# Layer 0 reads z and x with two neighbouring tokens per partition, and x for its moments in 32 KB per partition

## The chip, the cores and the metric

The kernel runs on one core of a Trainium2 chip. The metric is the device time of one execution in microseconds (us). Ten executions of the kernel before have a median of 3439.86 us (3437.83 to 3440.95).

## The reference

The input `x` is (1, 128, 256, 256): 128 rows s of 256 tokens i with 256 channels, in float32 (33.5 MB). Two attention layers are added to it in turn, each on a group-normalised input (32 groups of 8 channels, moments over all tokens). The change touches layer 0, which has a second input z, (256, 256, 128), also 33.5 MB:

```python
x = x + _L0_conv_ref(_gn(x), z, ...)
# in _L0_conv_ref, with 8 heads of 32 channels:
m_norm = layer_norm(m, ln_m_w, ln_m_b)
z_norm = layer_norm(z, ln_z_w, ln_z_b)
b = (z_norm @ Wb.T).transpose(0, 3, 1, 2)[:, None]     # a bias for each head, query i and key j
gate = sigmoid(m @ Wg.T + bg)
scores = einsum('bsihc,bsjhc->bshij', q, k) * scale + b
p = softmax(scores); o = einsum('bshij,bsjhc->bsihc', p, v) * gate
return o @ Wo.T + bo
```

The tokens of a row are exchangeable in the attention as long as queries, keys, bias and output use one order. Layer 1 is an attention limited to a band of 16 tokens to either side, so there the order of tokens matters.

## The kernel before, in words

`fast_kernel` does the work; a general kernel stands behind it for unusual inputs and isn't run here. It has three parts.

**The prelude** (lines 990 to 1140) works on z and on the moments of x. `z_front(b, i0)` (line 1048) loads a tile `zt` of 32 queries by 128 keys: partition p holds key b * 128 + p, and for each of 32 queries one run of 128 channels, 512 bytes. VectorE takes the moments of each query's channels (16 BATCH_NORM_STATS2, L1054), then the variance is scaled on VectorE (L1062) and GpSimd raises it to the power -1/2 (`zrs`, L1063). `z_back` (line 1068) transposes the tile on TensorE (L1077), ScalarE copies it (L1079), TensorE projects it to the heads (L1082); of every two tiles the result is turned back (L1092, `ps_k`), multiplied by `zrs` on VectorE in four pieces (L1098), biased on GpSimd (L1102) and exponentiated by ScalarE into `eb` (L1103), which is (128 keys, 8 heads, 2 key blocks, 256 queries). There are 16 such tiles, z0 to z15; `zt` has three buffers. `x_block(j)` (line 1109) loads 16 rows of x at once (4 MB, `xa`, two buffers): partition p holds tokens p and 128 + p of every row, 32 runs of 1 KB. VectorE takes the moments of pairs of groups (L1113, 16 instructions). The eight blocks are xa0 to xa7; `x_moments` (line 1116) merges them after the last.

The program's order of loads on SyncE's queue is z0, xa0, z1, z2, xa1, z3, xa2, z4, z5, xa3, z6, xa4, z7, z8, xa5, z9, xa6, z10, z11, xa7, z12 to z15. On each engine the order of the prelude's instructions is set by the framework's planner, from the costs it expects and the data each instruction needs, and then stays fixed. The buffers of the layer loop reuse the prelude's memory, so that its first load of x is issued after the last exponential into `eb`.

**Layer 0** goes through x in 64 pairs of rows, in an order written out by hand. `Pair` loads two rows (`xt`, L1179, five buffers), again token p and 128 + p of each row on partition p; it is normalised, transposed, projected to q, k, v and gate; `scores` and `add_bias` multiply the exponentials by `eb` (L1290); `apply`, `gate`, `out_row` and `keep_row` produce the new rows. Every 8 rows are stored to `x1` in HBM (L1360), and their moments taken for layer 1. `rows` is the access that lays token b * 128 + p on partition p.

**Layer 1** reads `x1` in pairs of rows (L1557) and writes `out`.

Of the kernel before, what the change touches and what calls it, by code (L numbers as in the profile page):

```python
# [10 lines left out]
AF = mybir.ActivationFunctionType  # L11
# [5 lines left out]
P = 128  # L17
# [4 lines left out]
def bcast(ap, axis, n):  # L22

    ap = ap.unsqueeze(axis)
    shape = list(ap.shape)
    shape[axis] = n
    return ap.broadcast_to(shape)
# [746 lines left out]
def fast_kernel(  # L774
# [25 lines left out]
    nc = tc.nc  # L800
# [7 lines left out]
    NB = I // P  # L808
# [94 lines left out]
    def rows(ap, s0, n):  # L903
        return ap[s0 : s0 + n].rearrange("s (b p) c -> p (s b) c", p=P)


    GA = min(16, S)

    eb = const.tile([P, H, NB, I], F32, name="eb")
# [9 lines left out]
    for a in range(KC):  # L919
        for h in range(H1):  # L920
            n = P // H1
# [11 lines left out]
    for h in range(H1):  # L933
        n = P // H1
# [22 lines left out]
    def group_pairs(src, g):  # L957

        return src[:, :, g * GE : (g + 2) * GE].rearrange("p n (h e) -> p n e h", h=2)
# [24 lines left out]
    with tc.tile_pool(name="pre", bufs=2) as pre, tc.tile_pool(  # L984
# [51 lines left out]

        IB, IS = 32, 64
        zjobs = [(b, i) for b in range(NB) for i in range(0, I, IB)]  # L1040
        wbz = pre1.tile([P, 4, 4, H], F32, name="wbz")
        nc.vector.memset(wbz, 0.0)
        for j in range(4):
# [2 lines left out]
        def z_front(b, i0):  # L1046

            nonlocal zrs
            zt = pre.tile([P, IB, CZ], F32, name="zt", tag="zt", bufs=3)
            nc.sync.dma_start(zt, z[i0 : i0 + IB, b * P : (b + 1) * P, :].rearrange("i p c -> p i c"))  # L1050

            st = pre.tile([P, IB, 3], F32, name="zst", tag="zst")
            for i in range(0, IB, 2):
                nc.vector.bn_stats(  # L1054
                    st[:, i : i + 2, :].rearrange("p i f -> p (i f)"),
                    zt[:, i : i + 2, :].rearrange("p i c -> p c i"),
                )
            at = i0 % IS
            if at == 0:
                zrs = pre.tile([P, IS], F32, name="zrs", tag="zrs", bufs=3)  # L1060
            rs = zrs[:, at : at + IB]
            nc.vector.tensor_scalar(rs, st[:, :, 2], 1.0 / CZ, 1e-5, ALU.mult, ALU.add)  # L1062
            nc.gpsimd.tensor_tensor(rs, rs, mhalf[:, :IB], ALU.pow)  # L1063
            return zt, zrs

        def z_back(b, i0, zt, rs):
            nonlocal ps_b
            at = i0 % IS
            if at == 0:
                ps_b = pps.tile([P, 512], F32, name="ps_b", tag="bias", bufs=1)  # L1070
            for j in range(at // 16, (at + IB) // 16):
                zTs = []
                for g in range(4):
                    ps_t = pps.tile([P, 512], F32, name="ps_t", tag="zT", bufs=3)
                    i = (4 * j + g) * 4 - at
                    for a in range(4):
                        nc.tensor.transpose(ps_t[:, a * P : (a + 1) * P], zt[:, i + a, :], ident)  # L1077
                    zT = pre.tile([P, 512], F32, name="zT", tag="zT", bufs=10)
                    nc.scalar.copy(zT, ps_t)  # L1079
                    zTs.append(zT)  # L1080
                for g in range(4):
                    nc.tensor.matmul(  # L1082
                        ps_b[32 * g : 32 * (g + 1), :], wbz[:, j].rearrange("p a h -> p (a h)"), zTs[g],
                        start=(j == 0), stop=(j == 3),
                    )
            if at + IB < IS:
                return
            bT = pre.tile([P, 512], F32, name="bT", tag="bT")
            nc.scalar.copy(bT, ps_b)
            ps_k = pps.tile([P, 4, 4, 4, H], F32, name="ps_k", tag="keys", bufs=1)  # L1090
            for a in range(4):
                nc.tensor.transpose(  # L1092
                    ps_k[:, a].rearrange("p g j h -> p (g j h)"), bT[:, a * P : (a + 1) * P], ident
                )
            bt = pre.tile([P, IS, H], F32, name="bt", tag="bt")
            for j in range(4):
                q = slice(j * 16, (j + 1) * 16)
                nc.vector.tensor_tensor(  # L1098
                    bt[:, q, :].rearrange("p (g a) h -> p g a h", g=4), ps_k[:, :, :, j, :].rearrange("p a g h -> p g a h"),
                    bcast(rs[:, q].rearrange("p (g a) -> p g a", g=4), 3, H), ALU.mult,  # L1100
                )
            nc.gpsimd.tensor_tensor(bt, bt, bcast(bz_r, 1, IS), ALU.add)  # L1102
            nc.scalar.activation(  # L1103
                eb[:, :, b, i0 - at : i0 - at + IS], bt.rearrange("p i h -> p h i"), AF.Exp
            )

        zrs = ps_b = None

        def x_block(j):
            xa = pre.tile([P, GA * NB, C], F32, name="xa", tag="xa")  # L1110
            nc.sync.dma_start(xa, rows(x, j * GA, GA))
            for g in range(0, G, 2):
                nc.vector.bn_stats(st0[:, j, g : g + 2, :].rearrange("p g f -> p (g f)"), group_pairs(xa, g))  # L1113

# [15 lines left out]
        for n, job in enumerate(zjobs):  # L1130
            front = z_front(*job)
            if behind is not None:
                z_back(*behind)
            behind = (*job, *front)
            if nx < nga and nx * 12 <= n * nga:
                x_block(nx)
                nx += 1
                if nx == nga:
                    M0, R0 = x_moments()
        assert nx == nga  # L1140
        z_back(*behind)


# [7 lines left out]
    x1 = [dram.tile([GB, I, C], F32, name=f"x1_{j}") for j in range(S // GB)]  # L1151
# [9 lines left out]
    with tc.tile_pool(name="l0", bufs=2) as sb, tc.tile_pool(  # L1161
# [10 lines left out]
        class Pair:  # L1172


            def __init__(self, p):
                self.p = p
                self.oT = {}
                self.xt = sb.tile([P, NT, C], F32, name="xt", tag="xt", bufs=5)
                nc.sync.dma_start(self.xt, rows(x, 2 * p, 2))  # L1179


            def centre(self):
# [169 lines left out]
            def keep_row(self, r):  # L1352
                s = 2 * self.p + r
                nc.vector.tensor_tensor(
                    xo[:, (s % GB) * NB : (s % GB + 1) * NB, :], self.ps_y.rearrange("p (b c) -> p b c", b=NB),
                    self.xt[:, r * NB : (r + 1) * NB, :], ALU.add,
                )
                if (s + 1) % GB == 0:
                    j = s // GB
                    nc.sync.dma_start(x1[j].rearrange("s (b p) c -> p (s b) c", p=P), xo)  # L1360
                    moments_of(xo, j)

        xo = None
        later = []

        def moments_of(src, j):

            new = st1 if j == 0 else sm.tile([P, G, 3], F32, name="gst", tag="gst", bufs=2)
            for g in range(0, G, 2):
                later.append(lambda g=g: nc.vector.bn_stats(  # L1370
                    new[:, g : g + 2, :].rearrange("p g f -> p (g f)"), group_pairs(src, g)))
            if j == 0:
                return
            d = sm.tile([P, G], F32, name="gd", tag="gd", bufs=2)
            d2 = sm.tile([P, G], F32, name="gd2", tag="gd2", bufs=2)
            each = float(GB * NB * GE)

            def merge():
                nc.vector.tensor_sub(d, new[:, :, 1], st1[:, :, 1])
                nc.vector.scalar_tensor_tensor(d2, d, each * j / (j + 1), d, ALU.mult, ALU.mult)  # L1380
                nc.vector.tensor_add(d2, d2, new[:, :, 2])
                nc.vector.tensor_add(st1[:, :, 2], st1[:, :, 2], d2)
                nc.vector.scalar_tensor_tensor(
                    st1[:, :, 1], d, 1.0 / (j + 1), st1[:, :, 1], ALU.mult, ALU.add
                )

            later.append(merge)
# [375 lines left out]
@with_exitstack  # L1763
def mixer_kernel(ctx, tc, *args):

    nc = tc.nc
    keep = ctx.enter_context(tc.tile_pool(name="verdict", bufs=1))
    verdict = keep.tile([1, 1], mybir.dt.int32, name="verdict")
    fast_kernel(tc, *args, verdict)
    again = nc.values_load(verdict[0:1, 0:1], min_val=0, max_val=1)  # L1770
    with tc.If(again > 0):
        general_kernel(tc, *args)
# [53 lines left out]
```

## Time and profile before

| | |
|---|---|
| median of 10 executions | 3439.86 us |
| the profiled execution | 3440.28 us, its span 3438.5 us |
| busy: TensorE, VectorE, GpSimd, ScalarE | 3259.1, 2020.2, 1983.0, 1454.9 us |
| z tiles: start of the first pass on VectorE | 27.57 us |
| starts of the eight x passes on VectorE | 40.30, 67.08, 91.42, 118.19, 133.29, 159.92, 184.06, 210.81 us |
| end of the last of them | 220.45 us |
| first load of x for layer 0 issued | 269.40 us |
| first scores of layer 0 | 308.84 us |
| read from and written to HBM | 188.82 MB, 68.75 MB |

The profile is of one execution. In its slices the span is cut in 40 equal parts of 86 us; a digit is a busy share in tenths. A group line gives the start, the length, the engine, the line, what is written from what, and in brackets how long the engine had been idle and what ended the wait. The prelude takes about a tenth of the span; the layer loops are TensorE's.

### The profile page before, as it was taken

To read this page: it belongs to the slowest core of one execution; us is meant where nothing else is said; L and a number is where in the kernel's file an instruction comes from. 1 tells how busy PE (TensorE), PEld (TensorE's weight loads), DVE (VectorE), ACT (ScalarE), POOL (GpSimd) and SP (SyncE) were. 2 spreads that over 40 slices of the span, in tenths; PEclk is the share of its full clock that TensorE was granted. 3 is DMA by queue.
4 is the path that set the end of the run, shared out by engine and by line. 5 is a ranking of instruction groups with operands and counts; after the bars stand their busy time and mean duration, and the time that the engine had idled before them with its cause. 6 is when DMAs were issued, how large, how long until landed. Compare 5 with 4: busy or idle time off the path is not lost. (4 is left out here: it accounts for less than half of the span.)

```text
span 3438.5 us, 81082 instructions
## 1 busy us (share of the span) xinstructions
PE 3259.1 (95%) x35158; PEld 2047.7 (60%) x35158; DVE 2020.2 (59%) x3218; ACT 1454.9 (42%) x2065; POOL 1983.0 (58%) x1385
## 2 busy tenths in 40 slices
PE   5565999999999999999999999799999999999998
PEld 3332555555555555555555555476767676777776
DVE  5872666666666666666666666366644444444455
ACT  2332444444444444444444444244444444444443
POOL 2445777777777777777777776333333333333332
PEclk8787999999999999999999999899999999999999
DMA  9971122122212221222122211221111212121211
GB/s 281 318 214 31 48 72 72 48 72 72 72 48 72 72 72 48 72 72 72 48 72 72 72 48 50 70 64 52 58 57 55 60 51 64 51 64 52 64 57 52
DMA packets 246941, 262.88 MB, mean 76 GB/s; under 512 B 46288, under 2 KB 213072, under 8 KB 246448
## 3 DMA queue, kind: packets, MB, share of 16 engines
q1 hardware_dynamic: 246576, 257.61, 26.0%
q8 instruction: 278, 4.55, 0.7%
q14 instruction: 87, 0.71, 0.1%
HBM read 188.82 MB, written 68.75 MB: 75 GB/s over the span
## 5 line engine op out<-in xcount | busy, mean ns | idle before, releaser
L1295 POOL TENSOR_TENSOR eboth<-e 128x512 f32<-128x512 f32 x512 | 639.7, 1271 | 401.8 <-DVE e L1290 401.8
L1290 DVE TENSOR_TENSOR e<-ps_sc,eb 128x1024 f32<-128x1024 f32 x512 | 603.2, 1220 | 338.8 <-ACT ps_sc L1281 253.7
L1281 ACT ACTIVATE ps_sc<-ps_sc 128x1024 f32<-128x1024 f32 x512 | 492.8, 1006 | 507.4 <-PE ps_sc L1274 507.4
L1615 POOL TENSOR_TENSOR e<-e,bw 128x384 f32<-128x384 f32 x256 | 258.9, 1033 | 443.9 <-ACT e L1613 443.9
L1576 PE MATMUL ps_p<-xgT,w_in 128*128 128x512 f32 x1024 | 469.6, 601 | 0.1
L1568 POOL TENSOR_TENSOR xt<-xt,bout_r 128x1024 f32<-128x1024 f32 x64 | 152.0, 2376 | 384.1 <-PE ps_x L1565 384.1
L1668 DVE TENSOR_TENSOR yo<-ps_y,xt 128x512 f32<-128x512 f32 x128 | 88.3, 690 | 378.6 <-PE ps_y L1664 378.6
L1576 PEld LDWEIGHTS ps_p<-xgT,w_in 128*128 128x128 f32 x1024 | 188.9, 190 | 200.0 <-issue 166.8
L1274 PE MATMUL ps_sc<-qT,kT 32*128 32x256 f32 x4096 | 293.8, 400 | 1.6 <-ACT kT L1244 1.6
L1240 PE MATMUL ps_p<-xnT,wq 128*128 128x512 f32 x512 | 255.7, 622 | 20.8 <-POOL xnT L1228 20.8
L1305 PE MATMUL ps_ov<-e,v 128*32 128x256 f32 x4096 | 274.1, 385 | 0.5 <-DVE oT L1319 0.5
L1240 PE MATMUL ps_p<-xgT,wg 128*128 128x512 f32 x512 | 253.9, 618 | 0.0
L1664 PE MATMUL ps_y<-w_out,oT 128*128 128x256 f32 x1024 | 248.6, 386 | 2.6 <-DVE oT L1649 2.6
L1347 PE MATMUL ps_y<-wo,oT 128*128 128x256 f32 x1024 | 243.8, 381 | 7.0 <-POOL oT L1337 7.0
L1347 PEld LDWEIGHTS ps_y<-wo,oT 128*128 128x128 f32 x1024 | 195.6, 191 | 88.0 <-issue 59.5
L1255 PE MATMUL ps_v<-wv,xnT 128*128 128x256 f32 x1024 | 242.1, 379 | 0.0
L1240 PE MATMUL ps_p<-xnT,wk 128*128 128x512 f32 x512 | 241.8, 595 | 0.0
L1274 PEld LDWEIGHTS ps_sc<-qT,kT 32*128 32x128 f32 x4096 | 185.4, 184 | 94.1 <-issue 70.5
L1591 PE MATMUL ps_v<-w_in,xgT 128*128 128x256 f32 x1024 | 231.8, 379 | 0.0
L1646 DVE RECIPROCAL rv<-odd 128x256 f32<-128x256 f32 x128 | 224.4, 1753 | 4.4
L1591 PEld LDWEIGHTS ps_v<-w_in,xgT 128*128 128x128 f32 x1024 | 194.4, 190 | 53.5 <-issue 30.1
L1255 PEld LDWEIGHTS ps_v<-wv,xnT 128*128 128x128 f32 x1024 | 189.6, 190 | 50.9 <-issue 31.1
(164 smaller groups left out, 5025.8 us busy)
## 6 DMA issues: line engine op xcount, KB each, us to landing
xa<-in_x_dram SPq DMA_DIRECT2D x8, 4096.0 KB
xt<-in_x_dram SPq DMA_DIRECT2D x64, 512.0 KB
rvb<-rsum SPq DMA_DIRECT2D x256, 128.0 KB
x<-xo SPq DMA_DIRECT2D x16, 2048.0 KB
xt<-x SPq DMA_DIRECT2D x64, 512.0 KB
out_dram<-yo SPq DMA_DIRECT2D x63, 512.0 KB
rs_r<-rs_d SPq DMA_DIRECT2D x64, 256.0 KB
rs_d<-lrs SPq DMA_DIRECT2D x64, 2.0 KB
```

Of the source, the lines that this page charges most:

```text
L1240: nc.tensor.matmul(ps, w[:, k, m * P : (m + 1) * P], getattr(self, src)[:, k, :], start=(k == 0), stop=(k == KC - 1),)
L1255: nc.tensor.matmul(self.ps_v[:, b * C : (b + 1) * C], self.xnT[:, k, t * P : (t + 1) * P], wv[:, k, :], start=(k == 0), stop=(k == KC - 1),)
L1274: nc.tensor.matmul(self.pss[q // 2][:, q % 2, b, :], self.kT[rs, c, r * I + b * P : r * I + (b + 1) * P], self.qT[rs, c, r * I : (r + 1) * I],
L1281: nc.scalar.activation(self.pss[a], self.pss[a], AF.Exp)
L1290: nc.vector.tensor_tensor(e, pss[a], eb[:, h : h + 2], ALU.mult)
L1295: nc.gpsimd.tensor_tensor(t, es[a][:, :, 0, :], es[a][:, :, 1, :], ALU.add)
L1305: nc.tensor.matmul(ov[q * D0 : (q + 1) * D0, :], self.v[:, r, b, h * D0 : (h + 1) * D0], es[q // 2][:, q % 2, b, :], start=(b == 0), stop= ...
L1347: nc.tensor.matmul(self.ps_y[:, b * C : (b + 1) * C], self.oT[r][:, k, b * P : (b + 1) * P], wo[:, k, :], start=(k == 0), stop=(k == KC - 1),)
L1576: nc.tensor.matmul(ps, w_in[:, k, n * C + m * P : n * C + (m + 1) * P], self.xgT[:, k, :], start=(k == 0), stop=(k == KC - 1),)
L1591: nc.tensor.matmul(ps[:, b * C : (b + 1) * C], self.xgT[:, k, t * P : (t + 1) * P], w_in[:, k, 2 * C : 3 * C], start=(k == 0), stop=(k == ...
L1615: nc.gpsimd.tensor_tensor(e[:, q], e[:, q], bcast(bw.rearrange("p b w -> p (b w)"), 1, KC), ALU.mult)
L1664: nc.tensor.matmul(ps[:, b * C : (b + 1) * C], self.oT[r][:, k, b * P : (b + 1) * P], w_out[:, k, :], start=(k == 0), stop=(k == KC - 1),)
```

## The change

Partition p now holds the neighbouring tokens 2p and 2p + 1 in layer 0, where it held p and 128 + p. In z, a tile takes 16 query pairs: its 32 columns are keys 2p and 2p + 1 of one query, for 16 queries of one parity (b), so that a run has 256 channels, 1 KB. A query's place in `eb` follows: even queries come first, then odd ones. The rows of x that the layer loop loads, and the rows of `x1` that it stores, have runs of two tokens, 2 KB. For the moments, which need no order, a block of 16 rows is laid out flat, 32 KB per partition. The bytes, tiles, buffers and the numbers of instructions on the compute engines stay. Layer 1 reads `x1` as before, since `x1` in HBM has the same content.

```diff
+        z_rows = z.rearrange("(u t) (p b) c -> t p u (b c)", t=NB, b=NB)
...
-            nc.sync.dma_start(zt, z[i0 : i0 + IB, b * P : (b + 1) * P, :].rearrange("i p c -> p i c"))
+            nc.sync.dma_start(
+                zt.rearrange("p (u b) c -> p u (b c)", b=NB), z_rows[b, :, i0 // NB : (i0 + IB) // NB, :]
+            )
...
             nc.scalar.activation(
-                eb[:, :, b, i0 - at : i0 - at + IS], bt.rearrange("p i h -> p h i"), AF.Exp
+                eb[:, :, :, b * P + (i0 - at) // NB : b * P + (i0 - at + IS) // NB],
+                bt.rearrange("p (u b) h -> p h b u", b=NB), AF.Exp,
             )
...
-            nc.sync.dma_start(xa, rows(x, j * GA, GA))
+            nc.sync.dma_start(xa, x[j * GA : (j + 1) * GA].rearrange("s i c -> (s i) c").rearrange("(p n) c -> p n c", p=P))
...
-                nc.sync.dma_start(self.xt, rows(x, 2 * p, 2))
+                nc.sync.dma_start(
+                    self.xt.rearrange("p (s b) c -> p s (b c)", b=NB),
+                    x[2 * p : 2 * p + 2].rearrange("s (p b) c -> p s (b c)", b=NB),
+                )
...
-                    nc.sync.dma_start(x1[j].rearrange("s (b p) c -> p (s b) c", p=P), xo)
+                    nc.sync.dma_start(
+                        x1[j].rearrange("s (p b) c -> p s (b c)", b=NB), xo.rearrange("p (s b) c -> p s (b c)", b=NB)
+                    )
```

## The prediction

> **What bounds the kernel now.** I read the slices of the page first. The transfer engines are full in the first slices alone, and there TensorE is half idle:
>
> ```profile
> PE   5565999999999999999999999799999999999998
> DMA  9971122122212221222122211221111212121211
> GB/s 281 318 214 31 48 72 72 48 72 72 72 48 72 72 72 48 72 72 72 48 72 72 72 48 50 70 64 52 58 57 55 60 51 64 51 64 52 64 57 52
> ```
>
> So the change, which alters transfers, can act in the prelude (z and the moments of x, some 300 us) and hardly elsewhere. Second, the table by stretches (columns after the length: busy us of PE, PEld, DVE, ACT, POOL, then TensorE clock, DMA share, GB/s). I cut the prelude where VectorE ends the last x block (220.45) and where the first x load of the layer loop is issued (269.40):
>
> ```profile
> 27.57:220.45 192.88, 116.91 (x630) 69.90 (x630) 147.68 (x357) 65.02 (x113) 72.56 (x18) 0.78 1.07 319
> 220.45:269.40 48.95, 30.86 (x174) 17.01 (x174) 26.98 (x90) 17.56 (x31) 29.58 (x7) 0.86 0.25 68
> 320.00:2160.00 1840.00, 1832.27 (x14228) 1060.04 (x14224) 1214.43 (x1945) 817.48 (x1014) 1438.28 (x1010) 1.00 0.23 63
> ```
>
> Stretch one: transfers always busy, VectorE 77%. Stretch two: transfers a quarter busy, no engine full, so a chain of waits. The layer loop: TensorE 99.6%, transfers 23%. Third, transfers of a stretch with only x under way (56 to 66 us), and of one with only z (42 to 47 us):
>
> ```profile
> DMA packets 3243, 3.45 MB, mean 345 GB/s; under 512 B 14, under 2 KB 3099, under 8 KB 3243
> DMA packets 723, 1.45 MB, mean 290 GB/s; under 512 B 16, under 2 KB 16, under 8 KB 723
> ```
>
> The 1 KB runs of x move at 345 GB/s, the 512 B runs of z at 290 (their records hold four runs each). A z tile is 128 x 32 x 512 B = 2.097 MB, 7.23 us; an x block 4.194 MB, 12.16 us. Last, VectorE in order of time, over one x block and the next, and its waits in 17 to 270 us (total, times, longest):
>
> ```profile
> 67.08 9.63 DVE L1113 BATCH_NORM_STATS2 st<-xa 128x6 f32<-128x512 f32 x16 [5.39 <-DMA xa<-in_x_dram]
> 76.63 5.39 DVE L1054 BATCH_NORM_STATS2 zst<-zt 128x6 f32<-128x256 f32 x16
> 85.09 0.29 DVE L1098 TENSOR_TENSOR bt<-ps_k,zrs 128x128 f32<-128x128 f32 x1 [3.06 <-PE ps_k L1092]
> 85.30 0.17 DVE L1062 TENSOR_SCALAR zrs<-zst 128x32 f32<-128x32 f32 x1
> 85.39 0.28 DVE L1098 TENSOR_TENSOR bt<-ps_k,zrs 128x128 f32<-128x128 f32 x1
> 91.02 0.49 DVE L1098 TENSOR_TENSOR bt<-ps_k,zrs 128x128 f32<-128x128 f32 x2 [5.35 <-POOL zrs L1063]
> 91.42 9.67 DVE L1113 BATCH_NORM_STATS2 st<-xa 128x6 f32<-128x512 f32 x16
> ...
> DVE bt L1098 <- POOL zrs L1063: 25.9, 6, 5.4
> DVE st L1113 <- DMA xa<-in_x_dram: 17.7, 3, 7.1
> DVE bt L1098 <- PE ps_k L1092: 12.1, 4, 5.5
> ```
>
> VectorE is the thread that leads to the end of stretch one, and its order is fixed. It waits for x three times, for the z projection ps_k (behind a z transfer) three times there, and for GpSimd's power (5.44 us each), which no transfer shortens. A faster stream is therefore worth much less than the time it saves on the transfer engines.
>
> **What the Trainium skill says.** "DMA: Bandwidth & Descriptors", section Why small descriptors are slow: each packet costs a fixed few cycles beside its beats, so short runs lose rate. The trace agrees: 290 against 345. Same page, section Measured: 341 GB/s for 1 MB, 425 for 16 MB. No x or z transfer here reaches that; the nearest, a 1 MB load in 8 KB rows (sums, 2189.2 to 2193 us), moves at 358 with the engines 95.7% busy, 374 if full. Same page, section Latency and other measured facts: row pitches of large powers of two cut the rate (half at 4 MiB); no transfer of before shows it.
>
> **The change, part by part.** Times are VectorE's starts of x blocks xa0 to xa7, before: 40.30, 67.08, 91.42, 118.19, 133.29, 159.92, 184.06, 210.81.
>
> *z in 1 KB runs.* Half the runs; I price them as today's 1 KB runs of x: 345 GB/s, 6.08 us instead of 7.23. Bounds: no gain (7.23), and 425 GB/s (4.93).
>
> *x blocks as 32 KB per partition.* Bounds: no gain (12.16), and 425 GB/s (9.87). I take 400, the mean of 374 and 425: 10.5 us. 4096 runs become 128, so SyncE's issue of 5.7 to 10.2 us a block should shrink; SyncE then waits at the buffers (two for x, three for z) instead, which holds nothing up, as the walk below shows.
>
> *Carried forward along VectorE.* Tile z0 lands 27.57 - 1.15 = 26.4. xa0: the old gap of 12.73 less 1.66, so 37.5. Before xa1 come z1 and z2, so xa1 lands 37.5 + 2 x 6.08 + 10.5 = 60.2; VectorE is free at 37.5 + (61.69 - 40.30) = 58.9, so it still waits 1.3: 60.2, 6.9 earlier. Tile z3 lands 66.3; its projection took 85.09 - 74.39 = 10.7 from landing to VectorE, so 77.0; the power and its wait follow as before (91.42 - 85.09 = 6.33): xa2 at 83.3, 8.1 earlier. From xa2 to xa3 26.77 us are two z tiles, 9.6 of x and two powers in a row on GpSimd (10.83): no transfer in it, 110.1. To xa4 15.10 likewise: 125.2. To xa5 26.63 less the 5.24 waited for x: 146.6 (the stream has it at 138.7). To xa6 24.14 less the 2.87 waited for ps_k: 167.8 (z9 lands 144.8, projected by 155.5; VectorE comes at 161.5). To xa7 26.75, again two powers: 194.6 against 210.81. **Gain 16.2 us.** Buffers: the block after next needs its VectorE pass done; xa4, the closest, needs xa2's pass (92.9) and has its turn in the stream at 105.6.
>
> *Stretch two, 48.95 us: unchanged.* After the last block come the merging of moments, two matmuls, a power, three more powers in a row (16.22 us), bias, exponential, the last projection and power. The last z tile is issued when z12 is released (237.9) and would land some 1.2 us sooner, but what follows it stands behind GpSimd until 254.5: no gain.
>
> *The exponential into eb* (L1103) writes pieces of 32 instead of 64, the same 512 elements: 1.13 us as now. If a piece doubled it, two of the eight lie in the tail: +2.3 us. The bias layout is otherwise the same size and its readers (L1290) have the same shapes.
>
> *x in pairs for the layer, 64 loads, and x1 stores, 16, in 2 KB runs.* The first load is on the path: 0.524 MB at 400 instead of 345 GB/s saves 0.2 us of the 4.45 from its issue (269.40) to GpSimd's start (273.85). The others, x1's stores included, lie under TensorE; waits for transfers between 400 and 2100 us sum to 1.2 us. If that cover went, the other 63 loads would bring 63 x 0.2 = 13 us more. The last x1 store overlaps the final moments. Layer 1 reads x1 as before.
>
> Sum: 16.2 + 0.2 = 16.4 us. The profiled execution was 3440.28 us (span 3438.5), the median 3439.86; 3440.28 - 16.4 = 3423.9, against the median 3423.5.
>
> **Rivals.** (a) *Only one transfer gains.* x at 12.16 with z at 6.08: the same walk gives xa1 63.5, xa2 86.6, xa5 149.9 and a gain of 12.9; z alone unimproved about the same: 3427. Were neither to gain, or the tail take it back: 3440. For it: the z runs' own spacing doubles; the 8 KB load shows only 374.
> (b) *The order changes.* Outside the layer loops the planner arranges each engine's instructions by the times it expects; before, it set the bias multiplies (L1098) ahead of the next x block. If it expects the new x earlier, blocks move ahead and the power waits (5.35, 4.55, 5.35, 4.91) hide. Then the stream decides: after xa5 at 138.7 come z9, x, z10, z11, x: xa7 at 178.0, a gain of 32.8, 3407. Against it: the bytes are unchanged. A partial shift lies between.
> (c) *Slower: the 32 KB rows collide in HBM.* All 16 transfer engines would walk rows at multiples of 32 KB in step, where now neighbouring partitions read neighbouring kilobytes. The stream becomes the bound: xa7 lands 26.4 + 11 x 6.08 + 0.6 + 8 t = 93.9 + 8t, which passes 210.81 at t = 14.6 us: under 287 GB/s the kernel is slower. At half today's rate, t = 24.3: +77 us, 3517. Against it: the 8 KB rows of sums, also contiguous as a whole, are not slow.
> (d) *The change does nothing to the end*, the transfers being hidden behind VectorE: then xa5 and xa1 would not wait for x, but they do, 5.24 and 5.39.
>
> **How the numbers follow.** My forecast 0.55 (3421 to 3428); (b) whole or part 0.20 (3404 to 3420); (a) weaker still or with a dearer tail, a gain of 1 to 12 us, 0.13; (c), or an order that lengthens the tail, 0.09; (d) 0.03. A fifth of a per cent, 6.9 us, is about what a measurement can tell: faster 0.83 (0.55 + 0.20 + 0.08 of (a)), same 0.08 (the rest of (a), and (d)), slower 0.09. The range 3404 to 3432 holds the forecast, most of (b) and half of (a): 0.80.
>
> **What would show it.** Right: x-only stretches near 400 GB/s and z-only near 345; xa7's pass at about 195; the issue of the first layer load near 253; the waits for GpSimd's power still 5 us each; the layer loop unchanged. Wrong: x-only under 345; VectorE's bias multiplies after the x blocks; a stretch two longer than 49 us; SyncE's waits between z tiles leaving the transfer engines idle before 180 us.

## The result, and the profile after

| | before | after |
|---|---|---|
| median of the runs, us | 3439.77 (28 runs) | 3427.02 (8 runs, 3424.77 to 3429.15) |
| ratio | | 0.9963 (95%: 0.9954 to 0.9972) |
| profiled execution, us | 3440.28 | 3428.09 |
| span of that execution, us | 3438.5 | 3426.3 |
| VectorE ends the last x block, us | 220.45 | 206.69 |
| first x load of the layer loop issued, us | 269.40 | 256.58 |
| first scores of layer 0, us | 308.84 | 294.94 |

The kernel became faster by 12.75 us, 0.37%; the forecast was 16.3 against these runs (3423.5). All of it was made before the layer loop began. On every engine the instructions stand in the same order as before; only the shapes of the exponential into `eb` (128x8x64 became 128x16x32) and of the transfers differ.

The table by stretches, cut at the same events as before (columns after the length: busy us of PE, PEld, DVE, ACT, POOL, then the share of its full clock that TensorE was granted, DMA share, GB/s):

```profile
27.78:206.69 178.91, 116.88 (x630) 66.13 (x630) 147.68 (x357) 63.15 (x113) 72.57 (x18) 0.80 0.94 346
206.69:256.58 49.89, 31.80 (x174) 17.00 (x174) 26.99 (x90) 17.44 (x31) 29.58 (x7) 0.78 0.13 43
310.00:2140.00 1830.00, 1828.10 (x14186) 1058.01 (x14184) 1209.70 (x1938) 815.07 (x1011) 1433.72 (x1006) 1.00 0.23 63
```

Stretch one is 13.97 us shorter (192.88 before). VectorE does the same work in it, 147.68 us, so only waiting went. The transfer engines are no longer always busy: their share fell from 1.07 to 0.94. By the packet records of the traces, the last of block xa7 landed at 204.65 us before and at 172.25 after, while VectorE took the block up at 210.81 and at 197.04: at xa7 the stream of transfers is 32.4 us ahead of the old one, and VectorE 13.8. Stretch two is 0.94 us longer (48.95 before). In the layer loop TensorE is busy 99.9% of the time.

Transfers of a stretch with only x under way (48 to 57 us), and of one with only z (36 to 46 us):

```profile
DMA packets 214, 3.81 MB, mean 423 GB/s; under 512 B 10, under 2 KB 100, under 8 KB 100
DMA packets 3388, 3.45 MB, mean 345 GB/s; under 512 B 20, under 2 KB 3388, under 8 KB 3388
```

An x block of 4.194 MB now takes 9.9 us (12.16 before) and a z tile of 2.097 MB 6.08 us (7.23 before). VectorE at one x block and just ahead of the next, and its waits between 17 and 310 us (total, times, longest):

```profile
59.59 9.67 DVE L1119 BATCH_NORM_STATS2 st<-xa 128x6 f32<-128x512 f32 x16 [0.55 <-DMA xa<-in_x_dram]
...
82.66 0.49 DVE L1103 TENSOR_TENSOR bt<-ps_k,zrs 128x128 f32<-128x128 f32 x2 [5.35 <-POOL zrs L1068]
...
DVE bt L1103 <- POOL zrs L1068: 26.6, 7, 5.4
DVE bt L1103 <- PE ps_k L1097: 11.7, 3, 6.7
DVE st L1119 <- DMA xa<-in_x_dram: 4.8, 2, 4.2
```

The waits for x fell from 17.7 to 4.8 us (the 5.39 before block xa1 became 0.55). The waits for GpSimd's power did not move: 26.6 us now, 25.9 before. The waits for `ps_k` hardly moved, 11.7 against 12.1; that is not what the forecast's walk had said.

Where VectorE starts the x blocks, us:

| | xa0 | xa1 | xa2 | xa3 | xa4 | xa5 | xa6 | xa7 | first layer load |
|---|---|---|---|---|---|---|---|---|---|
| before | 40.30 | 67.08 | 91.42 | 118.19 | 133.29 | 159.92 | 184.06 | 210.81 | 269.40 |
| forecast | 37.5 | 60.2 | 83.3 | 110.1 | 125.2 | 146.6 | 167.8 | 194.6 | 253 |
| after | 37.63 | 59.59 | 83.07 | 109.81 | 124.92 | 146.27 | 170.29 | 197.04 | 256.58 |

Up to xa5 the walk holds to 0.6 us. Between xa5 and xa6 it loses 2.75 us (24.02 instead of 21.27), and after xa7 about one more.

### The profile page after: what moved, and what is told of

The parts are those of the page before. It is cut to its first block, busy times and chain, and to the rows that moved or that the text cites. A ratio compares the mean times of both kernels' runs of the same rounds, so it can differ in the third digit from the quotient of the medians.

```text
span 3426.3 us, 81116 instructions
## 1 busy us (share of the span) xinstructions
PE 3260.5 (95%) x35158; PEld 2044.9 (60%) x35158; DVE 2019.9 (59%) x3218; ACT 1453.1 (42%) x2065; POOL 1982.9 (58%) x1385
```

## Where the missing time went: theories

Two traces leave two questions, and each got a theory and a rival.

*Why does a stream that saves about 37 us (16 z tiles by 1.15 us and 8 x blocks by about 2.3 us) bring 13?* Theory A: VectorE's fixed order, with its waits for GpSimd's power, uses up the rest. Theory B: the prelude's gain was larger, and the layer loop gave some back through its new transfers and the new order of `eb`.

*Why did the wait for `ps_k` before xa6 stay?* The forecast had put it down to the landing of z9, which came in time, at about 141.4. All engines in order of time, 138 to 172 us, after:

```profile
140.41 10.81 POOL L1068 TENSOR_TENSOR zrs<-zrs,mhalf 128x32 f32<-128x32 f32 x2 [9.89 <-DVE zrs L1067]
141.37 1.65 PE L1082 MATMUL ps_t<-ident,zt 128*128 128x128 f32 x12 [4.17 <-DMA zt<-in_z_dram]
...
151.19 1.26 POOL L1107 TENSOR_TENSOR bt<-bt,bz_r 128x512 f32<-128x512 f32 x1
...
152.48 1.06 ACT L1108 ACTIVATE eb<-bt 128x512 f32<-128x512 f32 x1 [16.39 <-POOL bt L1107]
...
154.07 1.11 PE L1082 MATMUL ps_t<-ident,zt 128*128 128x128 f32 x4 [11.06 <-ACT zT L1084]
...
163.17 0.66 PE L1097 MATMUL ps_k<-ident,bT 128*128 128x128 f32 x4 [0.68 <-ACT bT L1094]
163.96 0.29 DVE L1103 TENSOR_TENSOR bt<-ps_k,zrs 128x128 f32<-128x128 f32 x1 [2.77 <-PE ps_k L1097]
```

TensorE begins to transpose z9 at 141.37, does 12 pieces and then stands still for 11.06 us, because ScalarE does not copy them out of PSUM. ScalarE has been waiting 16.39 us at the exponential of the pair before (tiles z6 and z7), which needs GpSimd's bias addition, which stands behind two powers of 5.4 us. The copies of z9 are behind that exponential in ScalarE's queue, though they need nothing from it. So the wait is again one for the power, seen through ScalarE, TensorE and `ps_k`. Rival to this reading: the projection of z9 is late for a reason of its own, and the power on GpSimd only happens to run at that time.

## The experiments

**1. The layer loop's part alone.** The transfers of z and of the moments keep their old runs; the pairs in the layer's x, in x1 and in `eb` stay. Loop or prelude?

```diff
-        z_rows = z.rearrange("(u t) (p b) c -> t p u (b c)", t=NB, b=NB)
+        z_rows = z.rearrange("(u t) (p b) c -> t p b u c", t=NB, b=NB)
...
+            kb_, u0 = (i0 % IS) // IB, (i0 - i0 % IS) // NB
+            nc.sync.dma_start(zt, z_rows[b, :, kb_, u0 : u0 + IB, :])
...
-                bt.rearrange("p (u b) h -> p h b u", b=NB), AF.Exp,
+                bt.rearrange("p (b u) h -> p h b u", b=NB), AF.Exp,
...
-            nc.sync.dma_start(xa, x[j * GA : (j + 1) * GA].rearrange("s i c -> (s i) c").rearrange("(p n) c -> p n c", p=P))
+            nc.sync.dma_start(xa, rows(x, j * GA, GA))
```

> The changed kernel with both bulk loads put back: z again in runs of 512 B (but of neighbouring tokens, one parity of the keys in a tile), x for the moments again in 1 KB runs. What is left of the change is the 2 KB runs of the layer's x loads and x1 stores, and the pieces of 32 in the exponential. Theory A (the change acts on the prelude alone, along VectorE's order): no change but for 0.4 us in the first load, 3439 us, the x passes at the starts of the kernel before. Theory B (all the transfer time saved in the prelude, some 38 us, is gained and two thirds are given back by the layer loop, whose transfers are larger pieces): this kernel is some 20 us slower than before.

Measured: 3441.23 us, ratio 1.0005 (0.9997 to 1.0014), no difference that is clear of the noise; the median is 1.5 us above that of the kernel before. xa7 starts at 211.03 and the first layer load is issued at 269.62, as before the change. Theory B, which had some 20 us given back in the layer loop, falls. What the pairs in `eb`, in x and in x1 cost, if anything, is too small to be measured.

**2. x in 32 KB rows, z in 512 B runs.** The z part of the diff above, without its last edit.

> Of the two bulk loads the x blocks alone in 32 KB per partition; z in 512 B runs as in the run with neither. Theory A, walked along VectorE with 9.7 us for a block and 7.2 us for a z tile: xa1 62.0, xa2 86.3, xa5 149.6, xa7 near 200; a gain of 9 to 10.5 us, 3430. Theory B (gain in proportion to the stream's saving): x has saved 8 x 2.4 = 20 of some 38 us, so half the gain, 6.5 us.

Measured: 3430.63 us, ratio 0.9974 (0.9963 to 0.9984), 9.1 us faster than before. xa7 starts at 200.87.

**3. z in 1 KB runs, x blocks as before.** Only the last edit of the diff above.

> Of the two bulk loads z alone in 1 KB runs; the x blocks in 1 KB runs as before. Theory A, with 12.1 and 6.1 us: xa1 64.6, xa2 87.7, xa5 151.0, xa7 near 202; a gain of 8 to 9 us, 3431. The two gains do not add: each alone removes most of the waits for the stream. Theory B: 6.5 us, and the two add to the whole.

Measured: 3430.80 us, ratio 0.9975 (0.9965 to 0.9984), 8.9 us faster. xa7 starts at 199.78, and VectorE waits for x 9.2 us.

Each transfer alone brings some 9 us and both together 12.75, not 18. That fits theory A: the first improvement takes away most of VectorE's waits for x (17.7 us before, 7.2 in experiment 2, 9.2 in 3), so that the second finds few left, and the waits for GpSimd's power stay: 25.9 us before, 26.5 in experiment 2, 26.6 in 3, and 26.6 with both.

**4. One power fewer.** The power of tile z8 on GpSimd, the second of the pair that stands ahead of the bias addition at 151.19, is left out.

```diff
-            nc.gpsimd.tensor_tensor(rs, rs, mhalf[:, :IB], ALU.pow)
+            if (b, i0) != zjobs[8]:
+                nc.gpsimd.tensor_tensor(rs, rs, mhalf[:, :IB], ALU.pow)
```

> The changed kernel without GpSimd's power for the ninth z tile (z8), which leaves those bias rows scaled wrongly. It tells what holds up the projection of z9, which the prediction had taken as done in time. Theory A1 (ScalarE's queue: the exponential of tiles z6 and z7 stands ahead of z9's copies and waits for GpSimd, which has two powers before the bias addition): the exponential starts 5.4 us sooner, near 147, the wait of VectorE for the projection before xa6 goes, xa5 to xa6 falls from 24.0 to 21.3 us and the kernel gains 2.7 us on the changed one. Theory A2 (the z9 transfer is late): nothing changes, xa5 to xa6 stays 24.0.

Measured: 3423.97 us, ratio 0.9955 (0.9942 to 0.9969), 3.0 us below the changed kernel. The same part of the timeline, all engines (lines after L1068 are one number higher):

```profile
140.06 5.43 POOL L1069 TENSOR_TENSOR zrs<-zrs,mhalf 128x32 f32<-128x32 f32 x1 [9.88 <-DVE zrs L1067]
...
146.15 1.26 POOL L1108 TENSOR_TENSOR bt<-bt,bz_r 128x512 f32<-128x512 f32 x1 [0.67 <-DVE bt L1104]
...
147.45 1.06 ACT L1109 ACTIVATE eb<-bt 128x512 f32<-128x512 f32 x1 [11.76 <-POOL bt L1108]
...
149.03 1.11 PE L1083 MATMUL ps_t<-ident,zt 128*128 128x128 f32 x4 [3.82 <-ACT zT L1085]
...
157.09 0.66 PE L1098 MATMUL ps_k<-ident,bT 128*128 128x128 f32 x4 [0.68 <-ACT bT L1095]
160.80 0.29 DVE L1104 TENSOR_TENSOR bt<-ps_k,zrs 128x128 f32<-128x128 f32 x1
```

One power less on GpSimd, and the exponential on ScalarE starts 5.03 us earlier, TensorE takes up the transposes again 5.04 earlier, `ps_k` begins 6.08 earlier, and VectorE no longer waits for it. From xa5 to xa6 it is 21.22 us, which is the 21.27 of the forecast. xa7 starts at 193.86 (forecast 194.6) and the first layer load is issued at 253.05 (forecast 253). The reading by ScalarE's queue is shown, and the rival falls, since nothing of z9 itself was touched.

**5 and 6. The powers out of VectorE's way: the prelude in the order of the program.** If theory A holds, the change must be worth more in a prelude whose VectorE does not stand waiting for powers. The order of instructions is written out instead of planned, in both kernels; the merging of the moments goes ahead of the last tile's second half. Experiment 5 is the kernel before with this edit, 6 the kernel after with it.

```diff
-        for n, job in enumerate(zjobs):
+        with tc.manual_schedule():
+            for n, job in enumerate(zjobs):
...
-                if nx == nga:
-                    M0, R0 = x_moments()
...
-        z_back(*behind)
+            M0, R0 = x_moments()
+            z_back(*behind)
```

> The kernel before with the prelude's order written out by hand: on each engine the order of the program, in which the bias multiplies of a pair of tiles come after the next tile's pass, when GpSimd's power is long done, and the merging of the moments stands ahead of the last projection. VectorE then has no wait for a power and the stream decides: with 12.1 and 7.2 us, xa7 starts near 205.5 (it lands there in the kernel before too), its pass ends near 215, the first layer load is issued near 255. Theory A (power waits on VectorE's thread took the stream's gain): 3426, a gain of 14 us, most of it from the shorter end. A rival, that VectorE's own work (22 us per x block with two z tiles) is the bound: the same, so this run alone doesn't tell them apart; the next does.

> The changed kernel with the same order by hand. Theory A: the waits for the power being gone, the faster stream is worth more than in the planner's order: xa1 59.6, xa2 75.4, xa3 97, xa4 114, xa5 135, xa6 151, xa7 172 to 180, first layer load near 223 to 230, 3394 to 3402; against the run before, same order, a gain of 24 to 32 us where the planner's order gave 12.7. Rival (VectorE's own work is the bound with or without the waits): the gain stays near 13 us and xa7 starts near 190. A second wait may show, ScalarE's exponential standing before the next tile's copies.

Measured: 5 took 3441.41 us, ratio 1.0009 (1.0001 to 1.0018); 6 took 3411.94, ratio 0.9923 (0.9909 to 0.9936). VectorE's waits between 17 and 270 us, of 5 and then of 6:

```profile
DVE st L1113 <- DMA xa<-in_x_dram: 38.4, 8, 7.4
DVE bt L1098 <- PE ps_k L1092: 16.1, 3, 12.6
```

```profile
DVE bt L1103 <- PE ps_k L1097: 20.2, 5, 9.1
...
DVE st L1119 <- DMA xa<-in_x_dram: 6.3, 4, 4.2
```

The difference, which is what the two were for, came as theory A says: 29.5 us between 5 and 6, where 12.75 are had in the planned order. The rival, VectorE's own work as the bound, had the gain stay near 13 us. The waits for the power are gone from both lists; in 5 every one of the eight x blocks is waited for, in 6 these waits fall from 38.4 to 6.3 us. The absolute times were missed. In 5 xa7 starts at 205.94, 4.9 us ahead of the kernel before, but the first layer load is issued at 272.03, 2.6 us behind it. In 6 xa7 starts at 177.47 and the load is issued at 243.54. The written order was bad after xa7: the longest wait of 5 is 12.64 us, VectorE at the bias multiplies with `ps_k` not there. In 5 ScalarE's exponential at 228.00 us again stood ahead of the copies that `ps_k` needs, TensorE waiting 8.98 us for these, and the merging of the moments came late, from 252.69 us on.

**7 and 8. The same with the exponential out of the way.** The bias multiplies, the addition and the exponential of a tile are issued one tile later, and the moments are merged in steps between the last tiles. 7 is the kernel after with it, 8 the kernel before.

```diff
+        nx, pending, merge = 0, None, None
+        with tc.manual_schedule():
...
                 front = z_front(*job)
-                if behind is not None:
-                    z_back(*behind)
-                behind = (*job, *front)
+                ready = z_back(*job, *front)
+                if pending is not None:
+                    pending()
+                pending = ready
+                if merge is not None:
+                    MR = next(merge)
...
-                    M0, R0 = x_moments()
+                    merge = x_moments()
...
+            M0, R0 = MR
+            pending()
```

> The changed kernel in an order by hand as in the run before, with two waits of that run taken away: each tile's projection goes first and the pair's bias multiplies, addition and exponential a tile later, so that no exponential stands ahead of copies that the next projection needs; and the merging of the moments is laid in four steps between the last four tiles. Theory A: x passes where the stream brings them, xa7 at 172 to 177; first layer load near 226 (pass of xa7, four z passes of 5.5, 5 us of merging, the last power, addition and exponential); 3397, between 3392 and 3405, 22 to 35 us below the changed kernel. Rival (the end after xa7 is bound by TensorE at its low clock): first layer load no earlier than in the run before, 243, and 3412.

> The kernel before in the same order. Theory A: xa7 stays at 206, where the stream brings it; first layer load near 254 to 257; 3424 to 3428. So in this order the change is worth 26 to 31 us, as in the first order by hand, against 12.7 in the planner's. Rival: the worth of the change falls back to some 13 us, since the first order by hand had waits that favoured the changed kernel.

Measured: 7 took 3396.36 us, ratio 0.9868 (0.9853 to 0.9883), the fastest of all kernels here; 8 took 3430.85, ratio 0.9968 (0.9956 to 0.9980), some 3 us above the upper end of what was expected. The first layer load is issued at 226.75 in 7 and at 258.59 in 8. Stretch one of 7, then of 8 (cut at the same events, to 0.1 us):

```profile
28.00:182.50 154.50, 108.16 (x596) 62.18 (x595) 147.62 (x352) 59.30 (x107) 71.32 (x17) 0.83 1.04 386
```

```profile
28.00:215.50 187.50, 113.86 (x611) 68.31 (x612) 148.01 (x353) 61.48 (x109) 71.32 (x17) 0.79 1.07 320
```

Between the medians of 7 and 8 stand 34.5 us, of a stream that got some 37 shorter; the two traces show 31.8 of them at the first layer load. In 8 VectorE works 148.0 of 187.5 us, and the transfer engines are full: the stream sets the end. In 7 VectorE works 147.6 of 154.5 us, 96%, and the transfer engines are full as well (1.04). The last packet of xa7 landed at 172.23 us, and VectorE, which had just finished with a z tile, took the block up 0.7 us later:

```profile
172.30 0.70 DVE L1067 TENSOR_SCALAR zrs<-zst 128x32 f32<-128x32 f32 x1
172.93 7.27 DVE L1123 BATCH_NORM_STATS2 st<-xa 128x6 f32<-128x512 f32 x12
```

So VectorE's work and the stream are level in 7, and this run doesn't tell which of the two bounds stretch one.

The order alone, without the change, is worth 10.9 us (8), the change alone 12.75, both together 45.4. The order alone runs into the stream, and the change alone into the waits of VectorE's order.

## Why the prediction was right, and where it was not

**Bound and sign: right.** The change acted in the prelude alone. VectorE's order with its waits, and not the stream, set what it was worth: about a third of the time that the transfers saved. Experiments 1 and 5 to 8 show it, and so does xa7, which lay ready 24.8 us before VectorE came to it (6.2 before the change).

**The transfers.** z at 345 GB/s, taken from the 1 KB runs of x, came exactly. x came at 423 instead of 400, the middle of 374 and 425. The 374 is not the rate of 8 KB rows alone: in its window 391 of 511 packets were under 2 KB. The 425 stands in the Trainium skill, "DMA: Bandwidth & Descriptors", section Measured, for transfers issued from GpSimd, and these are issued from SyncE. The two rates of before would have done better, by an estimate: with 16 transfer engines at work, a run of 512 B at 290 GB/s takes 28.2 ns of one engine, and a run of 1 KB at 345 takes 47.5. That is 9 ns for each run and 26.6 GB/s for its bytes, and it puts runs of 32 KB at about 423.

The start xa0 = 37.5 was right by luck: two errors of 1.2 us cancelled. VectorE had z0 not 1.15 us earlier but at 27.78 (27.57 before), so that tile gained nothing; the x block behind it then took 9.85 us where the walk had 11.07, and xa0 fell at 37.63. By the packet records the rows of x had been moving since 25.0 us, while some 60 packets of 1 KB, z0's last among them, still came in from 26.0 to 27.3. Why these came late was not tried.

**The walk, xa0 to xa5: right** to 0.6 us, with the power waits in it unchanged.

**The walk, xa5 to xa6: wrong, 2.75 us.** The failing step is "24.14 less the 2.87 waited for ps_k ... (z9 lands 144.8, projected by 155.5)". It took the time from landing to projection of an earlier tile, 10.7 us, for z9. For z9 that path has a second condition, that ScalarE is free, and ScalarE was held by an exponential waiting on GpSimd. When the transfer came early enough, the same semaphore (the signal for which VectorE waits) was released by another chain at nearly the same time: 2.77 us waited instead of 2.87. Experiment 4 shows it: with one power less the walk's own figures return.

**Stretch two "48.95 us: unchanged": wrong by 0.94 us.** The forecast had named a stretch two over 49 us as a sign of being wrong, and it is 49.89. Its last projection ran slower. TensorE in order of time, after and then before:

```profile
243.31 2.40 PE L1087 MATMUL ps_b<-zT,wbz 128*32 128x512 f32 x4 [4.60 <-ACT zT L1084]
...
246.38 1.12 PE L1097 MATMUL ps_k<-ident,bT 128*128 128x128 f32 x4 [0.68 <-ACT bT L1094]
```

```profile
257.40 1.53 PE L1082 MATMUL ps_b<-zT,wbz 128*32 128x512 f32 x4 [2.76 <-ACT zT L1079]
...
259.61 0.65 PE L1092 MATMUL ps_k<-ident,bT 128*128 128x128 f32 x4 [0.68 <-ACT bT L1089]
```

The granted clock around these was 1.00 before (255 to 261 us) and 0.50 after (242 to 248), and the two groups took 1.34 us more (2.40 + 1.12 against 1.53 + 0.65). Less 0.33 us by which the projection began sooner after the last x block (36.62 us against 36.95), and 0.06 for a shorter exponential, that makes 0.95. The step that failed is "unchanged": it left the granted clock out.

Why the clock fell stays open. TensorE had idled 4.60 us ahead of these instead of 2.76. The Trainium skill, "TensorE: Matmul & The Clock Gate", Part 1, says that the clock falls to half after an idle window of about 3.4 us, and that the window runs freely, whatever the kernel does. These two traces agree with it, but the length of the gap doesn't decide alone. In experiment 1, with the old runs of z and x, the gap was shorter than in the kernel before, and the clock fell to 0.50 at 257.2 us all the same, in the middle of the projection:

```profile
256.46 2.23 PE L1086 MATMUL ps_b<-zT,wbz 128*32 128x512 f32 x4 [2.29 <-ACT zT L1083]
259.36 1.11 PE L1096 MATMUL ps_k<-ident,bT 128*128 128x128 f32 x4 [0.68 <-ACT bT L1093]
```

In experiment 2 it fell at 248.0 us, after a gap of 2.27. Of the kernel before, the kernel after and experiments 1 to 4, all in the planned order, only the kernel before had this projection at the full clock. So it isn't shown that the change made it slow. (In experiment 1 stretch two was still 48.9 us, as the projection began 1.2 us sooner after the last block.)

**The sum.** 16.2 less 2.44 (xa7 at 197.04 instead of 194.6) less 0.94 (stretch two) makes 12.8, and the first layer load was indeed issued 12.82 us earlier. Its way to GpSimd took 4.06 us instead of 4.45, a gain of 0.39 where 0.2 was forecast. The first scores came 13.9 us earlier and the profiled execution ended 12.19 earlier; the 1.7 us between those two are left open. From the first scores to the end the ten profiled executions of this document take 3128.6 to 3132.5 us, and those with the layer loop's old transfers alone 3128.6 (experiment 5) to 3131.9 (experiment 8), so that a cost of the new ones isn't shown.

**The exponential into `eb`**: no dearer with pieces of 32, 1066 ns against 1131 ns before.

**The rivals.** (a) gave the time, 3427, but not for its reason: both transfers gained, and experiments 2 and 3 put each alone at about 9 us, where (a) had 12.9. (b) falls, since the order is the same; yet its price was right in kind, for with the power waits out of the order, written by hand, the kernel goes to 3412 and 3396 (experiments 6 and 7), where (b) had 3407. (c) falls: 32 KB rows move at 423 GB/s, not under 287. The transfer engines do fall idle before 180 us, from about 178 on, which the forecast had named as a sign of being wrong; it cost nothing there, since xa7 had landed at 172.25. (d) falls, as the waits for x had said.

## What to carry to other kernels

A faster transfer is worth what the consumer's own thread waits for it, walked tile by tile with its other waits in place; here that was about a third of what the stream saved, and reordering the consumer made the same edit worth nearly three times as much. When a wait is struck out because its transfer comes sooner, look for the second condition of that semaphore: an engine that works in order and stands at an instruction for another tile holds up copies that are independent of it. Gains of two edits on one stream don't add, so run each alone before adding them.

## What the runs showed of the hardware that was not expected

- Runs of 512 B, 1 KB and 32 KB from HBM moved at 290, 345 and 423 GB/s on one core. All three fit some 9 ns of a transfer engine for each run, beside 26.6 GB/s for its bytes (an estimate from these rates). The 1 KB runs of z lie 256 KB apart in HBM and those of x before lay 128 KB apart; both moved at 345.
- GpSimd's power takes 5.44 us for 128x32 values, four times its bias addition on 128x512 (1.26 us). Two of these powers, 10.8 us, lay in the 16.39 us that ScalarE waited at one exponential; with one of them left out it waited 11.76.
- TensorE's last projection of z took 2.40 instead of 1.53 us at half the granted clock. The clock had fallen by the end of a gap of 4.60 us; in experiment 1 it fell after one of 2.29 us (2.23 us for the projection), and in the kernel before it didn't after one of 2.76. So the length of the gap alone didn't tell what the next work cost.
